# Two graph attention layers on one core: layer 1's reciprocals, cat's scaling and the projection moved to later steps

## The chip, the core and the metric

The kernel runs on one core of a Trainium2 chip. The metric is device time in microseconds, from launch to end, the median of several runs. A profile is one execution of its own, with its own time and a span from the first instruction to the last.

## The reference

Sixteen graphs of 1024 nodes with 256 features pass through two pre-norm attention layers. An adjacency matrix says which node may look at which; about 3% of its entries are 1, more for the first nodes.

```python
for layer in (0, 1):               # 4 heads of 64, then 8 heads of 32
    h = maximum(layernorm(x), 0)
    q, k, v = h @ Wq, h @ Wk, h @ Wv          # split into heads; layer 1 adds biases
    s = where(adj > 0, q @ k.T / sqrt(D), -inf)
    x = x + concat(softmax(s) @ v) @ Wo + bo
```

Everything is float32. The output is x after layer 1.

## The kernel before, in words

**Groups and steps.** All work is one hand-written stream of 768 steps. Layer 0 of batch b + 1 comes before layer 1 of batch b, so that one batch's projections can be made while another's attention runs. `first[b]` is the first step of layer 0 of batch b, `second[b]` that of layer 1. A layer is cut into four groups: two halves of 512 queries (`qh`), and in each two groups of heads (`g`), 128 rows of heads at a time. A group has 4 steps in layer 0 and 8 in layer 1. So layer 0 is 16 steps, layer 1 is 32.

**A step.** `scores` makes a block of 128 keys by 512 queries for each of four heads (or two keys blocks for two heads in layer 0) on TensorE into two of three PSUM buffers (line 400). VectorE takes the minimum with the mask and moves it to SBUF as `p` (line 416), ScalarE takes the exponential in place (line 421). Two steps later `weigh` multiplies by v on TensorE (line 433); `p` has seven buffers for even steps and two for odd ones. If a step with an even number has a projection due, its weigh is put off to the next step (line 490).

**Sums.** In layer 1, GpSimd adds the tiles of `p` up pair by pair (line 534) and by DMAs that add in memory (line 520, 1 MB each, issued by GpSimd's queue). A product with ones, `count`, gives the softmax sums (line 304). `brief` and `pairs` mark groups that count earlier: the last group of a layer, and the whole last layer.

**The end of a group.** `end_group` puts four things in the stream, counted in steps from the group's last weigh:

- `spread`: ScalarE copies the sums (line 320), and four SyncE DMAs lay them out over 128 lanes (line 333).
- `invert`: VectorE's reciprocal (line 341), a DMA to memory (line 343), and four that spread it to the rows of `inv` (line 346). `inv` has one buffer.
- `normalize`: GpSimd scales `cat` by `inv` (line 352).
- `end_half`, after the second group of a half: the projection with Wo (line 382), VectorE's sum with x (line 386), and for layer 1 the DMA to the output (line 388).

**Other work with due steps.** `later(i, f)` puts work on step i. Layer 1 of a batch and layer 0 of the batch after next get their norms (`stats` on VectorE, `norm` on ScalarE), `turn` (a transpose on TensorE), `k`, `q` and `values`. The mask of a batch comes in eight parts: `load` (line 128, GpSimd's queue, from memory, with a cast), `flip` (line 134, a DMA transpose on SyncE's queue, called the flip below) and `put` (line 143, a ScalarE copy into the mask). Both have one buffer, so a load waits for the flip before it, and a flip for the put before it. With c = second[b], the fifth to eighth parts of batch b + 2 have loads at c + 13 (and 12), 17, 21 and 25, flips at c + 15, 19, 23 and 27, puts at c + 17, 21, 25 and 29.

**Order.** Every engine, and SyncE's and GpSimd's DMA queues, run in the order in which the program issues. In a step, work is issued as: scores, weighs, counts, the exponentials, and then what is due in the order in which it was registered, TensorE's large pieces last. Set-up work is registered before the stream runs, a group's end during it. With second[b] = c, layer 1's groups weigh their last tile at c + 9, 17, 25 and 33. Their reciprocals stand before the change at c + 19, 27, 35 and 40, the scalings at c + 24, 32, 40 and 42, and the two projections at c + 34 and 44.

Of the kernel before, what the change touches and what calls it, by code (L numbers as in the profile page):

```python
# [82 lines left out]
def fast_program(ctx, tc, a, w, loads, chk):  # L83
# [375 lines left out]
    class Stream:  # L459
# [12 lines left out]
        def later(self, i, f, *args):  # L472
            self.due.setdefault(i, []).append((f, args))
# [84 lines left out]
        def end_group(self, i, gr):  # L558

            if gr.hurry:  # L560
                for f in (gr.spread, gr.finish, gr.inp.test):
                    self.later(i, f)
                return

            if gr.layer == 0:
                self.later(i + 4, gr.count_added)
                at = 4, 6, 8, 11
            else:
                at = (8, 10, 15, 17)
                if gr.pairs:  # L570
                    at = 2, 5, 7, 9
                elif gr.brief:
                    at = 4, 7, 9, 11
            for k, f in zip(at, (gr.spread, gr.invert, gr.normalize)):
                self.later(i + k, f)
            if gr.last:

                k = 7 if gr.layer or gr.inp.b == 0 else 37
                self.later(i + k if gr.inp.b + gr.layer < B - 1 else len(self.steps) + 2, gr.inp.test)
            if gr.g == 1:  # L580
                self.later(i + at[3], gr.end_half)
# [83 lines left out]
    later = stream.later  # L665

    def norms(inp, half, *at):

        for i, f in zip(at, (inp.stats, inp.stats, inp.norm, inp.norm)):
            later(i, f, half, (0, 1) if i in (at[0], at[2]) else (2, 3))  # L670
        later(at[3] + 1, inp.add_bias, half)

    def half_inputs(inp, half, *at):

        for i, f in zip(at, (inp.turn, inp.k, inp.q, inp.values)):
            later(i, f, half)
# [15 lines left out]
    for b in range(B - 1):  # L692
        mine, a, c = inputs[1][b], first[b + 1], second[b]
        if b == 0:

            norms(mine, 0, a + 5, a + 6, a + 8, a + 9)
            half_inputs(mine, 0, a + 11, a + 12, a + 14, a + 14)
            norms(mine, 1, a + 13, a + 14, a + 15, c)
            half_inputs(mine, 1, c + 1, c + 3, c + 6, c + 4)
        else:  # L700
            norms(mine, 0, a - 20, a - 19, a - 16, a - 15)
            half_inputs(mine, 0, a - 13, a, a + 4, a + 8)
            norms(mine, 1, a - 14, a - 10, a - 8, a - 6)
            half_inputs(mine, 1, a - 1, c, c + 6, c + 2)
        for i, u in zip((0, 2, 4, 6, 8, 10, 12, 13), range(NT)):
            later(a + i, masks[b].second, u)
        if b + 2 < B:
            other, mask = inputs[0][b + 2], masks[b + 2]
            later(a + 3, open_x, b + 2, 0)
            later(a + 13, open_x, b + 2, 1)  # L710
            if b == 0:
                norms(other, 0, a + 14, a + 15, c + 2, c + 3)
                half_inputs(other, 0, c + 5, c + 8, c + 16, c + 18)
                norms(other, 1, c + 3, c + 4, c + 6, c + 7)
                half_inputs(other, 1, c + 11, c + 22, c + 26, c + 30)
            else:
                norms(other, 0, a + 10, a + 12, a + 13, a + 15)
                half_inputs(other, 0, c + 1, c + 8, c + 16, c + 18)
                norms(other, 1, c, c + 4, c + 5, c + 6)
                half_inputs(other, 1, c + 9, c + 22, c + 26, c + 30)  # L720
            for i, t in zip((7, 12, 17, 22, 33, 37, 41, 45), range(NT)):
                later(a + i - 5 + (t > 4), mask.load, t)
                later(a + i - 2, mask.flip, t)
                later(a + i, mask.put, t)
        else:
            last, e = inputs[1][b + 1], c + 32
            norms(last, 0, c + 5, c + 6, c + 8, c + 9)
            half_inputs(last, 0, c + 11, c + 14, c + 16, c + 20)
            norms(last, 1, c + 13, c + 14, c + 16, c + 17)
            half_inputs(last, 1, c + 19, c + 24, e + 6, e + 4)  # L730
            for u in range(NT):
                later(c + 8 + 2 * u, masks[b + 1].second, u)
# [158 lines left out]
def kernel(  # L891
# [28 lines left out]
    with ExitStack() as fast, tc.manual_schedule():  # L920
        fast_program(fast, tc, a, w, loads, chk)
# [61 lines left out]
```

## Time and profile before

| | before |
|---|---|
| median of 3 runs | 3360.76 us (3353.34 to 3380.53) |
| profiled execution | 3366.5 us |
| its span | 3364.7 us |
| TensorE matmul busy | 3267.3 us, 97% of the span |
| VectorE busy | 2518.0 us, 75% |
| GpSimd busy | 2347.4 us, 70% |
| ScalarE busy | 2181.5 us, 65% |
| DMA accumulations, line 520 | 150 of 1024 KB, 8.4 us to landing |
| flips, line 134 | 3.3 us to landing in the median, 14.2 at most |
| sums, line 333 | 384 of 2 KB, 1.8 us to landing in the median, 7.6 at most |

PE, PEld, DVE, ACT, POOL and SP stand for TensorE's matmuls, its weight loads, VectorE, ScalarE, GpSimd and SyncE; a q after the name is the engine's instruction queue. `p<-mask,ps` reads: writes tile p from tiles mask and ps. In a group's line stand the count, then after the bar the busy time, the mean of one in ns, and after the next bar the time in which the engine stood idle just before, with what ended the wait. In a timeline a line has start, length, engine, source line, operation, tiles, count, and in brackets the idle time before it. A matmul's end is modelled, so TensorE can look busy where it isn't at its full pace.

### The profile page before, as it was taken

To read this page: it belongs to the slowest core of one execution; us is meant where nothing else is said; L and a number is where in the kernel's file an instruction comes from. 1 tells how busy PE (TensorE), PEld (TensorE's weight loads), DVE (VectorE), ACT (ScalarE), POOL (GpSimd) and SP (SyncE) were. 2 spreads that over 40 slices of the span, in tenths; PEclk is the share of its full clock that TensorE was granted. 3 is DMA by queue.
4 is the path that set the end of the run, shared out by engine and by line. 5 is a ranking of instruction groups with operands and counts; after the bars stand their busy time and mean duration, and the time that the engine had idled before them with its cause. 6 is when DMAs were issued, how large, how long until landed. Compare 5 with 4: busy or idle time off the path is not lost.

```text
span 3364.7 us, 44402 instructions
## 1 busy us (share of the span) xinstructions
PE 3267.3 (97%) x16990; PEld 1277.7 (38%) x16990; DVE 2518.0 (75%) x2760; ACT 2181.5 (65%) x2402; POOL 2347.4 (70%) x1244
## 2 busy tenths in 40 slices
PE   8999999999999999999999999999999999999898
PEld 3343333333433333343333433343343333433333
DVE  5776877768767787776877768777687777778876
ACT  6567576665756757667575665757667576674565
POOL 4578586775857758677585776857668586785776
PEclk9999999999999999999999999999999999999899
DMA  7348265472644826447273472736638365380431
GB/s 141 67 76 146 62 120 101 86 145 58 125 92 85 145 64 126 92 88 139 63 140 78 94 144 56 144 77 106 128 64 149 71 109 112 76 154 26 86 79 31
DMA packets 309453, 331.74 MB, mean 99 GB/s; under 512 B 189552, under 2 KB 257392, under 8 KB 290032
## 3 DMA queue, kind: packets, MB, share of 16 engines
q0 software_dynamic: 73824, 224.42, 37.1%
q1 hardware_dynamic: 235408, 104.41, 13.8%
q8 instruction: 135, 2.21, 0.3%
q14 instruction: 86, 0.70, 0.1%
HBM read 119.54 MB, written 17.56 MB: 41 GB/s over the span
## 4 chain that ended last, share of the span: by engine, by line
PE 77%; DMA 7%; ACT 5%; DVE 4%; POOL 3%; issue 2%; SPq 2%; DVEq 0%; ACTq 0%; POOLq 0%
PE ps L400 26%; PE po L433 23%; PE pq L225 11%; PE py L381 7%; PE pv L262 6%; PE pz L301 4%; DVE p L416 3%; DMA sums<-s 3%; DMA p<-p 3%; POOL p L534 3%; ACT p L421 2%; SPq L333 1%; DMA adjT<-adj 1%; ACT mask L143 1%; PE ph L208 1%
## 5 line engine op out<-in xcount | busy, mean ns | idle before, releaser
L421 ACT ACTIVATE p<-p 128x1024 f32<-128x1024 f32 x1536 | 1617.8, 1057 | 938.1 <-DVE p L416 892.4
L416 DVE SCALAR_TENSOR_TENSOR p<-mask,ps 128x1024 f32<-128x1024 fp8e4 x1536 | 1792.0, 1214 | 564.7 <-PE ps L400 547.8
L534 POOL TENSOR_TENSOR p<-p,p 128x2048 f32<-128x2048 f32 x255 | 1190.7, 4672 | 267.0 <-PE po L433 237.5
L400 PE MATMUL ps<-qT,kT 32*128 32x512 f32 (+1 forms) x6144 | 1187.2, 641 | 42.4 <-DVE p L416 40.8
L433 PE MATMUL po<-p,v 128*32 128x512 f32 (+1 forms) x6144 | 1003.0, 608 | 10.9 <-ACT p L421 10.3
L400 PEld LDWEIGHTS ps<-qT,kT 32*128 32x128 f32 (+1 forms) x6144 | 377.2, 186 | 739.0 <-issue 343.6
L446 POOL TENSOR_TENSOR p<-p 128x1024 f32<-128x1024 f32 x128 | 318.7, 2490 | 303.8 <-DVE p L445 298.8
L433 PEld LDWEIGHTS po<-p,v 128*32 128x32 f32 (+1 forms) x6144 | 230.0, 118 | 704.6 <-issue 521.9
L445 POOL TENSOR_TENSOR p<-p 128x1024 f32<-128x1024 f32 x64 | 151.4, 2366 | 263.5 <-DVE vn L341 162.0
L262 PE MATMUL pv<-wv,hT 128*128 128x256 f32 x1024 | 241.6, 390 | 14.5 <-ACT hT L209 14.5
L225 PE MATMUL pq<-hT,wk 128*128 128x512 f32 x512 | 239.9, 612 | 1.5 <-ACT hT L209 1.3
L381 PE MATMUL py<-wo,cat 128*128 128x256 f32 x1008 | 236.6, 388 | 2.3 <-ACT hT L209 1.0
L225 PE MATMUL pq<-hT,wq 128*128 128x512 f32 x512 | 236.6, 605 | 0.1
L262 PEld LDWEIGHTS pv<-wv,hT 128*128 128x128 f32 x1024 | 192.3, 193 | 91.5 <-issue 29.3
L381 PEld LDWEIGHTS py<-wo,cat 128*128 128x128 f32 x1008 | 188.5, 192 | 74.0 <-issue 48.6
L520 POOL DMA_DIRECT2D p<-p x150 | 150.9, 1006 | 40.2 <-POOL p L534 22.2
L352 POOL TENSOR_TENSOR cat<-cat,inv 128x512 f32<-128x512 f32 x127 | 169.2, 1332 | 12.3 <-DMA inv<-vd 8.9
L301 PE MATMUL pz<-p,ones 128*32 128x512 f32 (+1 forms) x1112 | 172.7, 595 | 0.8 <-ACT s L320 0.8
L448 POOL TENSOR_TENSOR p<-p,p 128x1024 f32<-128x1024 f32 x64 | 156.2, 2440 | 5.0
L143 ACT ACTIVATE mask<-adjT,mhalf 128x1024 fp8e4<-128x1024 bf16 x124 | 140.6, 1135 | 28.2 <-DMA adjT<-adj 28.1
L442 DVE TENSOR_TENSOR p<-p 128x1024 f32<-128x1024 f32 x128 | 156.0, 1218 | 0.0
L225 PEld LDWEIGHTS pq<-hT,wk 128*128 128x128 f32 x512 | 93.6, 193 | 146.9 <-issue 102.5
(50 smaller groups left out, 1688.6 us busy)
## 6 DMA issues: line engine op xcount, KB each, us to landing
p<-p POOLq DMA_DIRECT2D x150, 1024.0 KB, 8.4
adj<-in_adj_dram POOLq DMA_DIRECT2D x128, 256.0 KB, 4.1
x<-bo POOLq DMA_DIRECT2D x64, 512.0 KB, 5.9
x<-in_x_dram SPq DMA_DIRECT2D x32, 512.0 KB, 4.4
inv<-vd SPq DMA_DIRECT2D x128, 128.0 KB, 2.9
inv<-vd SPq DMA_DIRECT2D x252, 64.0 KB, 2.6
out_dram<-x SPq DMA_DIRECT2D x31, 512.0 KB, 3.0
sums<-s SPq DMA_DIRECT2D x384, 2.0 KB, 1.8
```

The source lines that it names most:

```text
L143: nc.scalar.activation(self.m[qh][:, :, ts(t % 4, P)], self.flipped.pop(t), AF.Identity, bias=w.mhalf[:, 0:1], saturate=False,)
L225: nc.tensor.matmul(pq[:, m, :], wt[self.layer][:, c, ts(m, P)], self.hT[half][:, c, :], start=(c == 0), stop=(c == 1),)
L262: nc.tensor.matmul(pv[:, i, :], self.hT[half][:, c, ts(i, P)], w.v[self.layer][:, c, :], start=(c == 0), stop=(c == 1),)
L301: nc.tensor.matmul(self.s[r * self.D : (r + 1) * self.D, :], w.ones[:, : self.D], p[:, r, :], start=start, stop=stop,)
L352: nc.gpsimd.tensor_mul(o, o, self.inv)
L381: nc.tensor.matmul(py[:, i, :], self.half.cat[:, c, ts(i, P)], w.o[self.layer][:, c, :], start=(c == 0), stop=(c == 1),)
L400: nc.tensor.matmul(st.ps[i // 2][:, i % 2, :], gr.inp.kT[r * D : (r + 1) * D, gr.g, ts(kt, P)], gr.inp.qT[gr.qh][r * D : (r + 1) * D, gr.g ...
L416: nc.vector.scalar_tensor_tensor(out=half, in0=gr.mask.m[gr.qh][:, kt, :].unsqueeze(1).to_broadcast([P, 2, 512]), scalar=BIG, in1=st.ps[i] ...
L421: nc.scalar.activation(half, half, AF.Exp, scale=gr.scale)
L433: nc.tensor.matmul(gr.o[r * D : (r + 1) * D, :], gr.inp.v[:, kt, h * D : (h + 1) * D], st.p[:, i, :], start=(kt == 0), stop=(kt == NT - 1),)
L446: nc.gpsimd.tensor_add(a, a, b)
L534: nc.gpsimd.tensor_add(one, one, st.p)
```

## The change

Three steps move; no instruction is added or taken away.

```diff
-                at = (8, 10, 15, 17)
+                at = (8, 12, 17, 19) if gr.qh == 0 else (8, 11, 14)
...
-            half_inputs(mine, 0, a - 13, a, a + 4, a + 8)
+            half_inputs(mine, 0, a - 13, a, a + 2, a + 8)
...
-            later(a + 3, open_x, b + 2, 0)
+            later(a + 5, open_x, b + 2, 0)
```

`at` holds the distances of spread, invert, normalize and end_half for groups of layer 1 that are neither `brief` nor `pairs`. In the first half, the reciprocals go from c + 19 and 27 to c + 21 and 29, the scalings from c + 24 and 32 to c + 26 and 34, the projection from c + 34 to c + 36. In the first group of the second half, the reciprocal goes from c + 35 to c + 36, and the scaling from c + 40 to c + 39. The layer's last group stays, and so does the last batch. With a = first[b + 1], which is 32 steps after the c of the batch before, layer 1's q of the first half goes from a + 4 to a + 2, so that it and the projection change places. The load of a new x goes from a + 3 to a + 5; it waits for the output DMA of the batch that had its buffer.

## The prediction

> **What bounds the kernel now.** I name steps as the code does: c = second[b] is the first step of layer 1 of batch b, a = c + 32 is where layer 0 of batch b + 2 begins, and "+19" is step c + 19. The views were read in this order: the page's chain of waits, windows by stage, the groups by line and form, the sources of lines 341 and 134, the timeline.
>
> ```profile
> PE 77%; DMA 7%; ACT 5%; DVE 4%; POOL 3%; issue 2%; SPq 2%; DVEq 0%; ACTq 0%; POOLq 0%
> ```
>
> TensorE carries 77% of the chain, DMA 7%. Where the DMA part sits is seen in windows cut by stage (length, then busy time and count of PE, PEld, DVE, ACT, POOL, then clock, DMA share, GB/s): two layer 0 stages, then the stretch from +17 to +31 in batches 1, 2 and 11.
>
> ```profile
> 1168.60:1250.20 81.60, 81.60 (x361) 31.84 (x361) 64.99 (x71) 43.94 (x49) 45.65 (x25) 1.00 0.25 59
> 1580.50:1662.10 81.60, 81.60 (x362) 31.83 (x360) 64.97 (x71) 43.95 (x49) 45.69 (x25) 1.00 0.30 69
> ...
> 484.40:534.90 50.50, 48.79 (x297) 18.39 (x296) 37.41 (x40) 40.44 (x47) 45.41 (x24) 1.00 0.90 162
> 688.00:747.60 59.60, 54.36 (x301) 19.83 (x300) 37.50 (x40) 40.91 (x47) 46.13 (x24) 0.89 0.83 150
> ...
> 2553.00:2606.80 53.80, 50.94 (x297) 18.89 (x296) 37.31 (x40) 40.42 (x47) 46.00 (x24) 0.97 0.83 150
> ```
>
> Layer 0 takes 81.6 us every time and PE never rests. The stretch from +17 to +31 has the same work in every batch and takes 50.5 to 59.5 us: something waits there. From the timeline, the other steps repeat to 0.02 us, so its undisturbed length can be added up from steps of equal content (2.07 us for a bare step, 2.92 after a delayed weigh, 4.7 with a projection): 46.1 us. The mean of the 14 stretches (b = 0 to 13) is 53.66 us (751.2 in all). So 14 x 7.6 = 106 us can be won at most, and nearly all that this kernel loses lies here.
>
> ```profile
> L341 DVE RECIPROCAL vn<-sums 128x16 f32<-128x16 f32 x63 | 15.7, 249 | 88.6 <-DMA sums<-s 88.4
> L341 DVE RECIPROCAL vn<-sums 128x8 f32<-128x8 f32 x64 | 12.5, 196 | 0.0
> ...
>   ACT mask L143: 28.1, 7
>   POOL adj L128: 8.9, 3
> ```
>
> The 16-column form is layer 1: 88.4 us of waiting in 28 waits, which the timeline puts at +19 and +27 of batches 0 to 13; layer 0's form never waits. The last two lines (source of line 134, who waited for it) are the second trouble: ACT's mask copy waited 28.1 us for the transposed adjacency.
>
> **What the Trainium skill says.** "TensorE: Matmul & The Clock Gate", section on architectural detail, calls ACT and DVE strict FIFOs: a reciprocal that waits holds every later line 416. The trace agrees: after the 1.77 us wait of batch 11, six of them run back to back (6.81 us). "DMA: Bandwidth & Descriptors", "Issuing engines are not separate DMA queues", says that DMAs of all engines run on the same 16 engines and interleave; "Queues, rings and completion order" says that they take turns packet by packet, from which a short transfer should slip past a long one. The trace agrees with the sharing, not with the slipping: a flip (line 134) issued 0.12 us after an accumulating p<-p landed in 8.7 us, right behind it; alone it takes 3.1. "Perfetto Trace Analysis", "Identifying the Most-Contended Engine", warns that matmul busy time is a poor measure: PE counts 50.9 us busy in these stretches for 46.1 of work.
>
> **The change, part by part.**
>
> *Reciprocals at +21 and +29 instead of +19 and +27.* No instruction is added. At +19 the last of the four sums lands 13.8 to 17.3 us after the start of step +17 (all times in this part count from there); two steps later DVE is ready at about 17.5, and at +29 well after the sums. So both waits end: 0 us, against 88.4. Behind the waiting instruction stood line 416, and behind that PE.
>
> *Its SP work moves too:* one vd and four inv issues. Batch 0, whose reciprocal ran at 17.48 because its sums were late, shows them at the new time: vd landed at 23.2 behind the p<-p of +20, inv was issued to 27.3 and landed at 31.3, while the next flip (+23) had to wait for its adj load until 30.9 in any case. So SP's flip is not delayed: 0 us, with 3.6 us in hand.
>
> *cat's scaling (line 352, POOL, 1.28 us) goes from +24 to +26.* This is the step that I think decides. On POOL it stood between line 534 of +23 and the p<-p issue of +25 (line 520), which races the flip of +23. In batch 11 and batch 1:
>
> ```profile
> 2582.85 1.28 POOL L352 TENSOR_TENSOR cat<-cat,inv 128x512 f32<-128x512 f32 x1
> 2584.07 0.90 POOL L520 DMA_DIRECT2D p<-p  x1
> ...
> 2584.20 1.27 SPq L134 DMA_TRANSPOSE adjT<-adj  x1
> ...
> 2592.95 1.15 ACT L143 ACTIVATE mask<-adjT,mhalf 128x1024 fp8e4<-128x1024 bf16 x1 [6.29 <-DMA adjT<-adj]
> ...
> 514.48 1.28 POOL L352 TENSOR_TENSOR cat<-cat,inv 128x512 f32<-128x512 f32 x1
> 515.71 0.89 POOL L520 DMA_DIRECT2D p<-p  x1
> ...
> 515.05 1.27 SPq L134 DMA_TRANSPOSE adjT<-adj  x1
> ...
> 518.44 1.14 ACT L143 ACTIVATE mask<-adjT,mhalf 128x1024 fp8e4<-128x1024 bf16 x1
> ```
>
> In batch 11 p<-p is first by 0.1 us and the mask waits 6.29 us; in batch 1 the flip is first by 0.7 and nothing waits. Over 14 batches: p<-p first in 2, 3 and 11 (mask waits 8.74, 6.31, 6.29); flip first by 0.45 in 8 (2.77); by 0.66 or more in the others (0 to 0.34). The losers are exactly the three with the shortest first wait (1.77 to 2.18 us): the stall that the change removes was holding p<-p back. With it gone, step +22 starts at 16.6 (17.3 in batch 11, 19.4 on average), line 534 of +23 ends at about 29.0, and without line 352 behind it p<-p goes at 29.6 to 30.9: once its predecessor has landed (29.1 to 30.9) and the count of +25 has run, 3.2 us into that step. The flip goes when adj has landed, 30.6 to 31.9, always 0.9 to 1.8 us after that same predecessor. So the flip loses everywhere. It lands 0.5 to 1.2 us after p<-p, which takes 7.4 to 10.4: at 39.3, and the mask, ready at about 33, waits 6 us in each batch: 84 us of new ACT waiting for 88.4 of old DVE waiting.
>
> *What that costs.* Behind the mask on ACT stand the copy of line 320 and the exponentials of +26, for which PE's weigh of +28 waits. In batches 2, 3 and 11 step +29 began 5.46 us after the mask copy. So +29 begins at 39.3 + 5.5 = 44.8 and, no reciprocal now holding DVE, +31 at 44.8 + 2.07 + 4.72 + 0.4 (DVE's 2.35 us a step over a bare step) = 52.0. **Sum: 14 x (53.66 - 52.0) = 23 us saved.**
>
> *POOL after it:* the next adj load waits for the flip, then line 352, then line 534 of +27 ends near 46.1, which line 416 of +29 needs (two odd p buffers) at 45.6: 0.5 us late, about covered by the 0.4 above.
>
> *The third group* (reciprocal +35 to +36, scaling +40 to +39) had no wait and gets no new one: in batch 9 its sums landed 3.2 us before the reciprocal, and inv 21.8 us before POOL's scaling, of which steps of 5.5 and 3.8 us are given up and 12 stay: 0 us. *q two steps earlier, end_half and open_x two later* in layer 0: q (3.70 us) and py (3.69) change places between two steps that both delay their weigh: 0 us, covered by PE being full; without that cover, DVE's 1.22 against 2 x 0.75 us. x still arrives some ten steps before its bn_stats. In batch 14 py and values now share step +36: up to 3.7 us, once; left out.
>
> The profiled execution took 3366.5 us (span 3364.7), 5.7 above the median of the runs; from the median: 3361 - 23 = **3338 us**.
>
> **The rivals.**
> - *Race lost, as above:* 0.58. A landing between 38.0 and 41.3 makes stretches of 50.7 to 54.0 us: 3320 to 3366.
> - *Race won:* p<-p goes after the flip, or the flip slips through in 3 us. For it: nine batches of fourteen win today, and gaps in POOL are partly irregular ("issue" 1.16 us in batch 11). Against: the order of the losers, and line 352 leaving. Stretch 46.1 + 1.3 for DVE and POOL (45.5 us busy) = 47.4: 88 us saved, 3273 us. Chance 0.18; some batches won and some lost, about 3305: 0.07.
> - *Slower:* ACT's wait costs more than DVE's did. One mechanism: the flip lands behind a p<-p that is as slow as in batch 2 (10.4 us). It decides from a landing at 41.0 on, where the stretch reaches 53.66. At batch 2's 42.3: 55.0, 14 x 1.3 = +19, 3380 us. For it: vd, inv and adj now land in the same 8 us. Against: two of three lost races landed by 39.9. Chance 0.17.
> - *The change does nothing:* the waits go along with the reciprocal. The landing of the sums doesn't depend on it, so under 0.01.
>
> **The numbers.** No change can be told within about 1% (34 us). Faster than 3327: the won cases (0.18, and 0.04 of the mixed) and the early end of the first (0.12), 0.34. Slower than 3394: half of the third, 0.09. The range of 8 in 10 leaves out half of the won case and that half: 3275 to 3384; the likeliest case alone is 3320 to 3366.
>
> **What would show it.** Line 341's wait on sums: under 5 us from 88.4. Line 143's wait on adjT: 70 to 90 us from 28.1, at +25, with line 520 issued before line 134; line 346's landing no new wait for line 352. Layer 0 stages: still 81.6. The stretch: 52 in every batch, with much less spread. If line 143 waits under 15 us, I am wrong on the race and the time is near 3273; if layer 0 grows, I am wrong on the part that I costed at nothing.

## The result, and the profile after

| | before | after |
|---|---|---|
| median, 9 runs each | 3358.99 us (3352.97 to 3380.53) | 3351.81 us (3348.46 to 3355.04) |
| ratio, 95% interval | | 0.9967 [0.9945, 0.9989] |
| span of the profiled execution | 3364.7 us | 3349.8 us |

The change makes the kernel faster by a third of a percent: 7 us between the medians, 15 us between the two profiled spans. That is less than half of the 23 us that the prediction expected, and within the 1% under which it held that no change can be told. The runs also lie much closer together: 6.6 us from end to end instead of 27.6.

The page's chain of waits by line, first in the kernel before, then in the kernel after, there by engine too:

```profile
PE ps L400 26%; PE po L433 23%; PE pq L225 11%; PE py L381 7%; PE pv L262 6%; PE pz L301 4%; DVE p L416 3%; DMA sums<-s 3%; DMA p<-p 3%; POOL p L534 3%; ACT p L421 2%; SPq L333 1%; DMA adjT<-adj 1%; ACT mask L143 1%; PE ph L208 1%
...
PE 81%; DMA 6%; POOL 5%; ACT 4%; DVE 3%; issue 2%; SPq 1%; ACTq 0%; POOLq 0%; DVEq 0%
PE ps L400 27%; PE po L433 25%; PE pq L225 11%; PE py L381 7%; PE pv L262 6%; PE pz L301 4%; POOL p L534 4%; DMA adjT<-adj 3%; ACT p L421 2%; DVE p L416 2%; DMA p<-p 2%; PE ph L208 1%; ACT mask L143 1%; ACT hT L209 0%; ACT s L320 0%
```

The sums are gone from the chain, and `adjT<-adj`, the flip, has risen from 1% to the 3% that they had. The groups by line and form show the exchange in numbers (busy and mean of one, then idle time before it and what ended it):

```profile
L143 ACT ACTIVATE mask<-adjT,mhalf 128x1024 fp8e4<-128x1024 bf16 x124 | 140.7, 1136 | 92.7 <-DMA adjT<-adj 92.7
L341 DVE RECIPROCAL vn<-sums 128x16 f32<-128x16 f32 x63 | 15.4, 245 | 0.0
```

The reciprocals waited 88.4 us and now wait for nothing. The mask copies waited 28.1 us and now wait 92.7. In the windows by stage (length, busy time and count of PE, PEld, DVE, ACT, POOL, then clock, DMA share, GB/s), first two layer 0 stages, then the stretch from +17 to +31 in batches 1, 2 and 11:

```profile
950.70:1032.30 81.60, 81.60 (x364) 31.86 (x364) 65.99 (x71) 43.94 (x49) 45.77 (x25) 1.00 0.30 70
1566.30:1647.80 81.50, 81.50 (x361) 31.79 (x360) 65.93 (x71) 43.84 (x49) 45.67 (x25) 1.00 0.31 72
...
482.50:534.50 52.00, 49.50 (x297) 18.64 (x296) 37.49 (x40) 40.02 (x47) 44.48 (x23) 0.97 0.82 145
687.60:740.50 52.90, 50.01 (x297) 18.75 (x296) 37.40 (x40) 40.13 (x47) 44.42 (x23) 1.00 0.80 143
...
2539.40:2592.60 53.20, 50.48 (x297) 18.89 (x296) 37.39 (x40) 40.08 (x47) 44.46 (x23) 0.97 0.81 144
```

Layer 0 is what it was. All 14 stretches lie between 51.6 and 54.0 us, where before they lay between 50.5 and 59.5; their sum went from 751.2 to 737.8 us. So 13.4 of the 14.9 us by which the span fell are here. Batch 1, which had won its race, got longer by 1.5 us; batch 2, which had lost, got shorter by 6.6. One such stretch, of batch 5, in the timeline (start, length, engine, line; the idle time before it in brackets):

```profile
1329.38 4.56 POOL L534 TENSOR_TENSOR p<-p,p 128x2048 f32<-128x2048 f32 x1
1334.76 0.92 POOL L520 DMA_DIRECT2D p<-p  x1 [0.82 <-PE po L433]
...
1344.55 0.61 POOL L128 DMA_DIRECT2D adj<-in_adj_dram  x1 [4.31 <-DMA adjT<-adj]
1345.18 1.29 POOL L352 TENSOR_TENSOR cat<-cat,inv 128x512 f32<-128x512 f32 x1
1346.41 4.54 POOL L534 TENSOR_TENSOR p<-p,p 128x2048 f32<-128x2048 f32 x1
...
1336.40 2.12 SPq L134 DMA_TRANSPOSE adjT<-adj  x1
...
1344.02 1.15 ACT L143 ACTIVATE mask<-adjT,mhalf 128x1024 fp8e4<-128x1024 bf16 x1 [6.27 <-DMA adjT<-adj]
...
1346.64 2.87 PE L433 MATMUL po<-p,v 128*32 128x512 f32 x8 [2.57 <-ACT p L421]
...
1350.98 2.35 DVE L416 SCALAR_TENSOR_TENSOR p<-mask,ps 128x1024 f32<-128x1024 fp8e4 x2 [4.52 <-POOL p L534]
```

The order of issue is to be read here. Line 520 follows line 534 directly, since the scaling (line 352) no longer stands between them. The flip comes 1.6 us after it, as adj has only then landed. It lands about 1 us after the 1 MB are through, and ScalarE has waited 6.27 us. TensorE then waits 2.57 us for the exponentials that stand behind the mask copy. GpSimd waits 4.31 us for the same flip before it may load the next part, does the scaling, and only then the addition of line 534, for which VectorE waits.

### The profile page after: what moved, and what is told of

Its sections match the earlier page's. It is cut to its first block, busy times and chain, and to the rows that moved or that the text cites. A ratio compares the mean times of both kernels' runs of the same rounds, so it can differ in the third digit from the quotient of the medians.

```text
span 3349.8 us, 44407 instructions
## 1 busy us (share of the span) xinstructions
PE 3254.1 (97%) x16990; PEld 1274.2 (38%) x16990; DVE 2530.3 (76%) x2760; ACT 2172.9 (65%) x2402; POOL 2349.8 (70%) x1244
## 4 chain that ended last, share of the span: by engine, by line
PE 81%; DMA 6%; POOL 5%; ACT 4%; DVE 3%; issue 2%; SPq 1%; ACTq 0%; POOLq 0%; DVEq 0%
PE ps L400 27%; PE po L433 25%; PE pq L225 11%; PE py L381 7%; PE pv L262 6%; PE pz L301 4%; POOL p L534 4%; DMA adjT<-adj 3%; ACT p L421 2%; DVE p L416 2%; DMA p<-p 2%; PE ph L208 1%; ACT mask L143 1%; ACT hT L209 0%; ACT s L320 0%
## 5 line engine op out<-in xcount | busy, mean ns | idle before, releaser
L400 PE MATMUL ps<-qT,kT 32*128 32x512 f32 (+1 forms) x6144 | 1165.0, 637 | 12.8 <-DVE p L416 11.3
L433 PE MATMUL po<-p,v 128*32 128x512 f32 (+1 forms) x6144 | 1016.4, 608 | 39.1 <-ACT p L421 38.1
L143 ACT ACTIVATE mask<-adjT,mhalf 128x1024 fp8e4<-128x1024 bf16 x124 | 140.7, 1136 | 92.7 <-DMA adjT<-adj 92.7
L225 PEld LDWEIGHTS pq<-hT,wk 128*128 128x128 f32 x512 | 93.0, 191 | 143.5 <-issue 94.1
```

Source lines behind the costliest of these rows:

```text
L143: nc.scalar.activation(self.m[qh][:, :, ts(t % 4, P)], self.flipped.pop(t), AF.Identity, bias=w.mhalf[:, 0:1], saturate=False,)
L225: nc.tensor.matmul(pq[:, m, :], wt[self.layer][:, c, ts(m, P)], self.hT[half][:, c, :], start=(c == 0), stop=(c == 1),)
L400: nc.tensor.matmul(st.ps[i // 2][:, i % 2, :], gr.inp.kT[r * D : (r + 1) * D, gr.g, ts(kt, P)], gr.inp.qT[gr.qh][r * D : (r + 1) * D, gr.g ...
L433: nc.tensor.matmul(gr.o[r * D : (r + 1) * D, :], gr.inp.v[:, kt, h * D : (h + 1) * D], st.p[:, i, :], start=(kt == 0), stop=(kt == NT - 1),)
```

## The experiments

Ten kernels were run, each beside runs of the kernel before on the same chip. Theory A throughout is that of the prediction: the flip of +23 loses a race to the accumulating DMA of +25. B says that the DMA engines are full and order has no meaning, C that GpSimd is the bound.

| run | median us | ratio to before, 95% | wait on adjT, us | wait on sums, us | the 14 stretches, us |
|---|---|---|---|---|---|
| before (the profile shown) | 3358.99 | | 28.1 | 88.4 | 751.2 |
| the change | 3351.81 | 0.9967 [0.9945, 0.9989] | 92.7 | 0 | 737.8 |
| e1 order, all groups | 3387.05 | 1.0092 [1.0054, 1.0131] | 107.7 | 7.3 | 769.0 |
| e2 first scaling back | 3321.86 | 0.9878 [0.9845, 0.9910] | 28.2 | 0 | 705.8 |
| e3 scaling alone | 3371.23 | 1.0018 [1.0004, 1.0032] | 55.0 | 104.8 | 758.9 |
| e4 before, order | 3509.37 | 1.0438 [1.0403, 1.0473] | 96.3 | 175.2 | 886.0 |
| e5 order, third group | 3390.96 | 1.0082 [1.0058, 1.0106] | 108.5 | 1.3 | 677.3 |
| e6 load before the DMA | 3323.39 | 0.9872 [0.9852, 0.9893] | 6.5 | 0 | 722.7 |
| e7 scaling later | 3343.20 | 0.9937 [0.9916, 0.9958] | 90.9 | 0 | 727.8 |
| e8 third group undone | 3352.03 | 0.9962 [0.9949, 0.9976] | 94.1 | 0.5 | 736.1 |
| e9 = e6 and e7 | 3301.75 | 0.9807 [0.9788, 0.9827] | 3.6 | 0 | 684.5 |
| e10 = e9, DMA behind the load | 3299.27 | 0.9798 [0.9778, 0.9818] | 10.4 | 6.4 | 671.5 |

The waits and stretches are those of each run's one profile. The kernel before took 3363.94 us beside e1 to e4, 3364.51 beside e5 to e8 and 3368.07 beside e9 and e10, so the ratios compare better than the medians.

### e1: the accumulating DMA behind the addition, in every group

```diff
-                if not (gr.brief or gr.pairs) and j == 7:
-                    self.accumulate(gr.two, gr.one)
                 nc.gpsimd.tensor_add(one, one, st.p)
+                if not (gr.brief or gr.pairs) and j == 7:
+                    self.accumulate(gr.two, gr.one)
```

> The change, and besides it the accumulating p<-p DMA of a group's eighth tile (line 520) is issued by GpSimd after the tile addition of line 534 instead of before it. Theory A (the flip at +23 loses a race to that DMA in the queue): line 520 goes some 4.6 us later, at about 34 us after step +17 begins, when the flip has landed; line 143's wait on adjT falls from 92.7 us to under 15, the stretch from +17 to +31 from 52.7 us to about 48, so about 3352 - 14 x 4.7 = 3286 us. Rival B (the DMA engines are full in this stretch, and the order only decides where the wait shows): the waits on adjT stay over 60 us in all or turn up on inv or sums, the stretch stays at 51 to 53 us, 3340 to 3356 us. Rival C (GpSimd binds: it is busy 44.7 us of the stretch): the adjT wait goes, but the stretch stops near 50, about 3315 us.

It came out slower, and none of the three had said so. The wait left +25 altogether, as A has it, but the edit also delays the DMA of the group before, at +17, and with it the adj load that the flip of +19 needs. Batch 5 in the timeline:

```profile
1336.80 0.90 POOL L520 DMA_DIRECT2D p<-p  x1 [0.81 <-PE ps L400]
...
1337.68 1.48 SPq L134 DMA_TRANSPOSE adjT<-adj  x1
...
1347.15 1.15 ACT L143 ACTIVATE mask<-adjT,mhalf 128x1024 fp8e4<-128x1024 bf16 x1 [7.15 <-DMA adjT<-adj]
```

This is the same race one flip earlier: that flip now goes 0.88 us after the DMA of +20 and lands 9.4 us later, in all 14 batches (98.3 us of wait at +21). A's mechanism holds, but the expectation was wrong by 101 us because it looked at one race and not at the one beside it.

### e4: the same edit in the kernel before

> The kernel before with the one change of order of the first of these runs. Theory A: batches 2, 3 and 11 lose no race any more; their stretches of 59.5, 56.6 and 53.8 us fall to about 51.5, and the waits for sums stay: line 341's wait about 70 us, line 143's under 8, about 3359 - 16 = 3343 us. Rival B (order doesn't matter): 3359 us, adjT wait as before (28 us).

A missed by 166 us. The flips of +23 won in every batch, but those of +19 and +27 lost, and the sums, now issued behind a DMA in flight, landed later: the reciprocals, still two steps behind their copy, waited 175.2 us. So order is worth far more here than the change under study, which B can't explain.

### e5: the same edit in the third group alone

```diff
+                first = not gr.qh
-                if not (gr.brief or gr.pairs) and j == 7:
+                if first and not (gr.brief or gr.pairs) and j == 7:
                     self.accumulate(gr.two, gr.one)
                 nc.gpsimd.tensor_add(one, one, st.p)
+                if not first and not (gr.brief or gr.pairs) and j == 7:
+                    self.accumulate(gr.two, gr.one)
```

> The change, with the p<-p DMA after the addition of line 534 in the second half's group alone, so that the flip at +19 keeps its head start. Theory A: line 520 of +25 goes at about 34 us after step +17 begins; the flip at +23 wins, and the mask copy at +25 waits under 2 us. But the adj load of +25 and the p<-p of +28 are then both gated by that later DMA (landing near 43), so the race can move to the flip at +27: if that one wins, a stretch of 48.5 us and about 3293 us; if it loses, the mask copy at +29 waits 5 us or more from +30 on, and 3310 to 3350 us. Rival B (full DMA engines, order without meaning): the wait stays at +25, over 60 us, 3340 to 3356 us.

The wait at +25 fell to 26 us over the 14 batches and the stretches to 48.4 us each, as A has it, and the race moved to the flip of +27, which A had named as the danger. Batch 5 in the timeline:

```profile
1357.84 1.41 POOL L520 DMA_DIRECT2D p<-p  x1
...
1357.96 1.28 SPq L134 DMA_TRANSPOSE adjT<-adj  x1
...
1366.24 1.15 ACT L143 ACTIVATE mask<-adjT,mhalf 128x1024 fp8e4<-128x1024 bf16 x1 [5.71 <-DMA adjT<-adj]
```

0.12 us behind, and ScalarE waits 5.71 us. The price was higher than expected (3391 us, not 3310 to 3350). This wait ends at the border to layer 0: step +31 took 5.0 us more than in the change, layer 0's first step 1.7, and the wait is outside the stretch that the table adds up.

### e6: the adj load ahead of the DMA of +21

```diff
                 elif j == 3:
-                    self.accumulate(one, gr.one)
+                    if gr.qh and not gr.g:
+                        self.later(i, self.accumulate, one, gr.one)
+                    else:
+                        self.accumulate(one, gr.one)
```

> The change, with the adj load of +21 issued ahead of the p<-p DMA of +21 in GpSimd's queue instead of behind it; nothing else moves. Theory A: the load lands near 25 us after step +17 begins instead of 31, the flip of +23 goes when SyncE is through with inv, near 27.5, 2.5 us and more before the p<-p of +25; line 143's wait on adjT falls from 92.7 us to under 15, the stretch from 52.7 to about 48 us, 3352 - 14 x 4.7 = 3286 us. Rival B (full DMA engines): something else waits in its place, the stretch stays over 51 us, 3335 to 3356 us. Rival C (GpSimd binds): adjT wait gone, stretch 49.5 to 51, 3305 to 3325 us.

This takes the cause away instead of moving it. In batch 5:

```profile
1319.59 0.88 POOL L128 DMA_DIRECT2D adj<-in_adj_dram  x1
1320.25 1.09 POOL L520 DMA_DIRECT2D p<-p  x1
...
1330.66 0.94 POOL L520 DMA_DIRECT2D p<-p  x1 [2.65 <-PE ps L400]
...
1326.38 2.23 SPq L134 DMA_TRANSPOSE adjT<-adj  x1
```

The flip goes 4.3 us ahead of the DMA of +25, and 6.5 us of wait are left of 92.7. A's mechanism is shown by this run: nothing but the order of two issues was changed, and B's 3335 to 3356 us is out. A's size is not reached (3323 us, not 3286): the second line 520 above stands 2.65 us until its predecessor has landed (its bracket names a matmul; over the whole trace the profile puts 33.6 us of line 520's waits down to p<-p itself), GpSimd falls behind, and line 416 waits for line 534 with its tile of +29, while TensorE is at +30 (24.3 us in all). TensorE then worked 3.4 us at half its clock in 13 of 14 batches. The time is C's (3305 to 3325 us), the mean stretch of 51.6 us is not (49.5 to 51): GpSimd's delay costs something here, but that its total work is the bound is not shown.

### e2 and e3: the two halves of the change

e2 leaves the first group's scaling at +24; e3 leaves the reciprocals where they were.

```diff
-                at = (8, 12, 17, 19) if gr.qh == 0 else (8, 11, 14)
+                at = (8, 12, 17 if gr.g else 15, 19) if gr.qh == 0 else (8, 11, 14)   # e2
+                at = (8, 10, 17, 19) if gr.qh == 0 else (8, 10, 14)                   # e3
```

> The change, but the first group's scaling of cat stays at +24, where it was. Theory A: the scaling stands in GpSimd's queue ahead of line 520 again, and it must now wait for inv, which lands near 31 us after step +17 begins, so line 520 goes at 32.5 or later and the flip, at 31 to 32, wins in most batches: line 143's wait on adjT under 30 us, the stretch about 48.5 us, about 3293 us. Rival B (full DMA engines): the flip lands late whatever the order, wait on adjT over 60 us, 3340 to 3360 us. Rival C (GpSimd binds): its 2 us wait for inv costs about what the flip's wait did, 3330 to 3345 us.

> The change without its moved reciprocals: they stay at +19, +27 and +35; scalings, projection, q and the load of x move. Theory A: the wait of the first reciprocal still holds back line 520, but line 352 no longer does, so the races of batches 4 and 7, perhaps 8, are lost besides those of 2, 3 and 11; each costs some 6 us, as the second reciprocal then waits for sums behind the mask copy; line 341's wait over 88 us, line 143's 35 to 50, 3365 to 3380 us. Rival B (order doesn't matter): 3359 us as before, 28 us of wait on adjT.

e2: no batch loses its race; line 520 goes at 32.7 to 34.3 us after step +17 begins, and the flip at 30.9 to 32.7. GpSimd pays for it with 40.3 us of waiting for inv at that scaling, of which little reaches TensorE: stretches of 50.4 us instead of 52.7, a kernel 1.2% faster than before. That is between A's 3293 and C's 3330. e3: eight batches lose instead of three (2, 3, 7, 8, 9, 11, 12 and 13); A had named five or six. Both waits go up, and it is a little slower than before. So neither half brings the 14 losses alone: the reciprocals' stall had been holding line 520 back, and the scaling as well (in e2 for longer than before, since inv lands later there).

### e7 and e8: what the steps behind the race cost, and the parts costed at nothing

e7 takes the first group's scaling on to +30; e8 puts the third group back to +35 and +40.

```diff
-                at = (8, 12, 17, 19) if gr.qh == 0 else (8, 11, 14)
+                at = (8, 12, 17 if gr.g else 21, 19) if gr.qh == 0 else (8, 11, 14)   # e7
+                at = (8, 12, 17, 19) if gr.qh == 0 else (8, 10, 15)                   # e8
```

> The change, with the first group's scaling at +30 instead of +26, so that it no longer stands between the flip's landing and line 534 of +27. It tells what the steps from +29 to +31 cost, which the prediction set 0.8 us too low per stretch. Theory A1 (GpSimd's late line 534 holds VectorE through the two odd p buffers): line 416's wait on line 534 falls from 45.9 us to under 20 and each stretch by about 0.5 us, some 7 us in all, 3345 us. Theory A2 (TensorE's clock, granted at half for a few us after it stood idle 2.6 us): the wait on GpSimd falls, the time stays within 3 us of the change, since the steps with a low clock don't get shorter. In both the adjT wait stays at 85 to 100 us.

> The change without its part for the first group of the second half: reciprocal at +35 and scaling at +40 again. Every theory of the prediction costs that part at nothing: the same time as the change within 3 us, about 3352 us, the adjT wait at 85 to 100 us, layer 0 stages at 81.6 us.

The waits of line 416 for line 534 (total, times, longest), after and in e7:

```profile
DVE p L416 <- POOL p L534: 45.9, 41, 4.8
```

```profile
DVE p L416 <- POOL p L534: 20.1, 35, 2.4
```

e7: the stretches lose 10 us in all, the median is 8.6 us lower, and the wait at +29 (27.7 us in the change) is gone. That is A1's 3345 us. A2's "no shorter" is out: beside e8, which differs from the change in the third group alone, e7's stretches are shorter both where TensorE's clock fell to half in them (52.5 against 52.9 us on average) and where it didn't (51.4 against 52.1). e7 also has fewer of the first kind, 7 against 9, so a part of its gain may still come from the clock. e8: 3352.03 us and about the same waits, so the third group's part is worth nothing that these runs can tell.

### e9 and e10: what the runs point to

e9 is e6 with e7's scaling; e10 also puts the DMA of +25 behind line 534 and the load of +25.

```diff
-                at = (8, 12, 17, 19) if gr.qh == 0 else (8, 11, 14)
+                at = (8, 12, 17 if gr.g else 21, 19) if gr.qh == 0 else (8, 11, 14)
...
                 if not (gr.brief or gr.pairs) and j == 7:
-                    self.accumulate(gr.two, gr.one)
+                    if gr.qh:                                     # e10 only
+                        self.later(i, self.accumulate, gr.two, gr.one)
+                    else:
+                        self.accumulate(gr.two, gr.one)
```

> The two edits that the runs so far favour, on top of the change: the adj load of +21 ahead of the p<-p DMA of +21, and the first group's scaling at +30. With the load first alone, no wait on adjT was left but GpSimd fell behind: line 416 waited 24.3 us for line 534 at +30, and TensorE then worked 3.4 us at half its clock in 13 of 14 batches, a step of 8.5 us where 4.7 would do. Theory A (GpSimd's lag, by way of the two odd p buffers, then the low clock): taking the 1.3 us of line 352 out of GpSimd's way there removes most of that; line 416's wait at +30 under 8 us, step +30 about 5.5 us, the stretch 48 to 49 us, about 3290 us. Rival C (GpSimd binds by its total of 45 us): the lag only moves on, the stretch stays at 50.5 or more, 3312 to 3325 us.

> As the run before it, and the p<-p DMA of +25 is issued behind line 534 and the adj load of +25. GpSimd then doesn't stand for 2.65 us at +25 until the p<-p of +21 has landed. Theory A: the load of +25 lands at 37 instead of 41, the flip of +27 can't lose its race, line 534 of +27 ends near 40.5, the stretch 47.5 to 48.5 us, 3278 to 3290 us. Rival B (full DMA engines): the later accumulation makes the p<-p of +28 and the counts late, TensorE waits at the next layer 0, which grows over 81.6 us; 3300 us or more.

The same windows of e9, batches 1, 5 and 11:

```profile
478.20:526.70 48.50, 48.49 (x297) 18.66 (x296) 37.48 (x40) 40.51 (x47) 43.20 (x22) 1.00 0.92 161
1285.90:1334.70 48.80, 48.79 (x301) 18.71 (x300) 37.48 (x40) 40.59 (x47) 43.31 (x22) 1.00 0.89 155
2500.50:2549.10 48.60, 48.59 (x301) 18.71 (x300) 37.48 (x40) 40.46 (x47) 43.25 (x22) 1.00 0.87 155
```

PE fills the stretch and the clock is 1.00. The DMA share is higher than ever (0.87 to 0.92), so the same traffic goes through in less time: B is out. The stretch is the 48 to 49 us that A named, and C, which set 50.5 or more, is out too. The kernel takes 0.9807 of the time of before, some 1.5% less than the change; the time lies 12 us above A's, on a chip whose runs of the kernel before gave 3368 us. In e10 the stretches fall to 48.0 us, but layer 0 grows in most batches, by up to 1.2 us, as B had said, and VectorE waits at +31 for GpSimd: 2625.7 us lie outside the stretches instead of 2615.2. Between e9 and e10 the intervals overlap: e10 isn't clearly better, and A's 3278 to 3290 us were not reached.

## Why the prediction was right, and where it was too high

- **What shows it.** The time alone doesn't: the median of the kernel before, 3358.99 us, lies in the same 3320 to 3366 us of the likeliest case. The waits and landings that follow do.
- **The bound** stood as read: all variation lay in the 14 stretches, and layer 0 kept its 81.6 us. The undisturbed 46.1 us were reached by no run: the shortest stretch of all, in e10, took 47.9, which would leave 81 us to win and not 106.
- **Reciprocals at +21 and +29:** 0 us of waiting, as forecast.
- **SP's moved work:** the flip went at 30.8 to 32.9 us, against the forecast's 30.6 to 31.9. What set it was adj's landing, as the prediction had it; in some batches that came up to a microsecond later. (In the kernel before, the flip followed the landing of the DMA of +21 by 0.7 to 1.9 us, not 0.9 to 1.8; nothing hung on it.)
- **The race:** line 520 went at 29.6 to 31.2 us (29.6 to 30.9 forecast), the flip lost in all 14 batches and landed at 39.4 on average (39.3 forecast). The wait at +25 came to 89.9 us (84 forecast). e6, e5 and e1 show that the order of issue decides, not the traffic alone.
- **What the wait costs:** step +29 began at 44.7 us on average (44.8 forecast).
- **The term that was mis-sized** is the last one: from +29 to +31 the prediction set 2.07 + 4.72 + 0.4 = 7.2 us, and it took 8.0. So a stretch took 52.7 us and not 52.0; times 14 that is 10 of the 23 us, and leaves the 13.4 that the stretches saved. The prediction had seen line 534 of +27 come out 0.5 us late and called that "about covered by the 0.4 above". VectorE waited about 2 us a stretch for it, and e7 shows that this wasn't covered: with the scaling out of GpSimd's way these two steps took 7.7 us, and +29 began 0.4 us earlier. The rest wasn't taken apart; even e9, at full clock, took 7.8.
- **The median that it was taken from.** The saving was counted in the profiled execution of the kernel before, which took 3366.5 us, 7.5 above the median of its nine runs, and was then taken off a median. The profiled execution of the change, 3351.91 us, stands at its median. That is why the spans differ by 14.9 us and the medians by only 7.
- **Parts costed at nothing:** the third group by e8, and q, end_half and open_x by the unchanged 81.6 us. The two projections that meet in batch 14 cost nothing that can be seen: its layer 1 took 130.5 us instead of 132.2.
- **The spread:** the kernel before lost a race in some batches and won it in others. Now all are lost alike, and the runs lie within 6.6 us. That the races are the cause of the spread between runs is only argued, since each kernel was profiled once. For it: e3, with some lost and some won, spreads over 29.6 us in 20 runs, e9, with all won, over 0.8 in four. Against: e6, with all won too, over 17.7 in four.

## What to carry to other kernels

A wait that goes lets everything behind it start earlier, also what was better late: before taking a stall away, list what its engine issues next and which transfers it will then overtake. Where a short transfer and a long one are issued within a few microseconds of each other, give the short one's source its place ahead of the long one, as e6 does, rather than moving a scaling that happens to stand between them. And look at the races on both sides of the one that is mended: e1 and e5 lost more there than they won.

## What the runs showed of the hardware

A flip issued after a 1 MB accumulating DMA landed only with it or just after it, even 0.1 us behind: 8.3 us to landing in e5's batch 5, against 3.1 in batch 1 of the kernel before, where it was 0.7 us ahead. The traces of before, the change, e1, e2, e3, e5, e7 and e8 hold 112 flips of +23. The 58 that went 0.66 us or more ahead of the DMA of +25 landed in 3.0 to 4.6 us, the 53 that went behind it in 6.4 to 15.0, and the one that led by 0.45 us in 6.0. What in the DMA engines makes it so, no run shows.

TensorE's granted clock fell to half in spells. Batch 10 of the change shows one, first in the timeline of PE and then in two windows with the clock in the third column from the end:

```profile
2370.87 1.14 PE L400 MATMUL ps<-qT,kT 32*128 32x512 f32 x8
2375.22 2.87 PE L433 MATMUL po<-p,v 128*32 128x512 f32 x8 [3.21 <-ACT p L421]
2378.01 2.09 PE L400 MATMUL ps<-qT,kT 32*128 32x512 f32 x8
```

```profile
2370.90:2374.50 3.60, 1.11 (x12) 0.28 (x8) 3.13 (x3) 1.91 (x3) 1.36 (x2) 0.92 0.34 65
2374.50:2381.30 6.80, 6.08 (x24) 1.09 (x24) 1.09 (x1) 6.38 (x8) 6.80 (x5) 0.54 0.46 79
```

The same eight matmuls take 1.14 us before the gap and 2.09 after it. The length of the gap alone doesn't tell whether the clock falls. In the change's profile, its start apart, every gap of TensorE from 2.07 us on had a spell at it except one of 2.89; but in e7 gaps of 2.18, 2.52, 3.02 and 3.05 us had none, in the kernel before one of 1.45 us had one, and in e6 the clock fell 13 times with no longer gap than 0.92 us just before. The clock records of the 12 traces show more. In each trace all spells begin on one fixed grid of 3.413 us, to within 0.02 us, and last 1 to 4 of its cells, where the end of the program doesn't cut them short. After every one of the 115 cells at full clock in which TensorE was busy, by the modelled ends of its matmuls, for less than 0.4 of the cell (the first 68 us of each trace apart), the next cell was at half. After those busy for more than 0.6 it was so in 17 of 11081, 14 of them in e6, which stay unexplained; in between, in 38 of 83. So how a gap lies on the grid counts, and not only how long it is.

A wait on TensorE can thus cost more than its own length, which the forecast's 2.07 and 4.72 us, steps at full clock, leave out. In the change, e7 and e8 the stretches with a spell took 0.5 to 1.1 us more on average than those without; how much of that is the longer wait itself was not taken apart.
